# Moving one turn's older values and routing places between the two batches' scores, and one attention step ahead of the last transposes

## The chip, the cores and the metric

The kernel runs on one core of one Trainium2 chip. The metric is the device time of one execution, in microseconds (us); lower is better. The core has five engines that each take their instructions in the order in which they were written and wait for one another through semaphores: PE (TensorE, matrix products and transposes), DVE (VectorE), ACT (ScalarE), POOL (GpSimd) and SP, which here issues transfers.

## The reference

The program is a gated cross-attention block followed by a mixture of experts, for 8 batches of 256 queries, width 128, 16 heads of 64, and 1601 keys. Cut to what matters:

```python
q = (layernorm(x) @ Wq + bq)            # 16 heads of 64
k = ctx @ Wk + bk ; v = ctx @ Wv + bv
scores = q k^T / 8 ; masked ; causal    # a query sees only keys up to its own place
x = x + tanh(g_xattn) * (softmax(scores) @ v @ Wo + bo)
y = layernorm(x)
indices = argmax(softmax(y @ Wr + br))  # one expert of 8 for each token
for i in range(8):
    xi = y * (indices == i)
    out += relu(xi @ W1[i] + b1[i]) @ W2[i] + b2[i]
x = x + tanh(g_ffn) * out
```

Because of the causal mask only the first 256 keys matter (a query whose visible keys are all masked gets the mean of all values, which is why the kernel also sums the other keys).

## The kernel before

Batches are taken in 4 pairs and heads in 8 pairs, so there are `NG` = 32 turns, `g` = 0 to 31: turn `g` is pair `g // 8` of batches with pair `g % 8` of heads. Everything is float32. The loop over `g` is written out as a hand-made order (`tc.manual_schedule()`): each engine executes what the source lists, in that order, and a step that waits holds up all later steps of its engine.

One turn is spread over three passes of the loop. In pass `g` the scores of turn `g` are made; in pass `g+1` its probabilities are normalized; in pass `g+2` they are transposed and multiplied with the values. The helpers are:

- `biases(g)`: 8 small products on PE, four for each bank, that put the mask into two PSUM banks, `banks[0]` for the pair's first batch and `banks[1]` for its second (L522). They have to wait until the exponentials of turn `g-1` have read the bank.
- `scores(g, b)`: 8 source-level products on PE for batch `b` (L541, each shown twice in the trace because float32 takes two passes), then the negated row maxima on DVE: one reduction (L549) and two custom instructions (L551).
- `exps(g, b)`: four exponentials on ACT (L572), each with the reading of its row sum.
- `normalized(g, b)`: reciprocals of the row sums on DVE (L586), then two multiplications on POOL (L595).
- `turn(g, i)`: three transposes on PE (L603) into one of two PSUM buffers `pt`, and a copy out on DVE (L605). `i` is 0 to 3: batch `i // 2`, head `i % 2`.
- `values(g)`: eight products of transposed probabilities and values on PE (L616) into a PSUM buffer `o`, and for the last four turns its eviction on ACT (L637) into the tile `att` (shown as `arena`).
- `router_places(p)`: for the four 128-token tiles of a pair, 14 small bfloat16 products on PE (L716 to L720) into a buffer `n`, then five small DVE instructions (L721 to L726) that turn the counts into places of the experts' rows. `scatter` (L741) later sends rows to these places from POOL.
- `misc` is a ring of two PSUM buffers that queries, keys, values, `o`, `n` and the last outputs share.

Pass 30 (`NG - 2`) ends with `biases(30)`, `scores(30, 0)`, `exps(30, 0)`, `scores(30, 1)`, `values(28)`, `router_places(2)`. Then pass 31 begins with `turn(29, 0)`, `turn(29, 1)` and `a.out(0..3)`: the output products of the last pair for the first batch (`a`, a `Half`; the second batch is `b`), into the buffer `y_last0`, which takes the place in the ring that `o` of turn 28 has left (L779). `exps(30, 1)`, `turn(29, 2)`, `turn(29, 3)`, `normalized(30, 0)`, `normalized(30, 1)` and turn 31's own biases, scores and exponentials follow, then `values(29)`.

After the loop, `last_turns` writes out the rest. There `a.attend(g)` is `values` for one batch (L616 into the bank `sc_0`, eviction on ACT at L795), `a.out(c)` adds head pair `c`, and `plan(n)` issues the next `n` of 18 small DVE instructions (L1054) that plan the first experts' loads. It is followed by the routing of the last pair and by the experts (L986 first layer, L994 its activation, L1002 second layer, L1020 the rows' way out).

Of the kernel before, what the change touches and what calls it, by code (L numbers as in the profile page):

```python
# [53 lines left out]
def tile_gated_xattn_moe(  # L54
# [4 lines left out]
    nc = tc.nc  # L59
# [14 lines left out]
    def misc(name):  # L74
        return ps_m.tile([P, 512], F32, tag="misc", name=name)
# [188 lines left out]
    def gates():  # L264
        nc.scalar.activation(tg, g_sb, AF.Tanh)
# [213 lines left out]
    NG = NC * NPAIR  # L479
# [50 lines left out]
    def scores(g, b):  # L530

        q, k, s = qT[g], kT[g], banks[b]
        for t, at in enumerate((K0, K1)):
            for u in range(2):
                n = HB * (BLOCK[t][u] + 1)
                for j in range(2):
                    r = slice(DK * j, DK * (j + 1))
                    lo = b * S + t * P + HB * u  # L540
                    nc.tensor.matmul(  # L541
                        s[HB * u : HB * (u + 1), j, at : at + n],
                        lhsT=q[r, lo : lo + HB],
                        rhs=k[r, b * S : b * S + n],
                        start=(t == 1),
                        stop=True,
                    )
        m = nmax[g, b] = p4.tile([P, 2, 2], F32, tag="nmax", name=f"nmax_{g}_{b}")
        nc.vector.tensor_reduce(m[:, 0], s[:, :, U0:K1], AX.X, ALU.max, negate=True)  # L549
        for j in range(2):  # L550
            nc.vector.tensor_tensor_reduce(  # L551
                out=s[:, j, K1:U1],
                in0=s[:, j, K1:U1],
                in1=bias[:, 2 * (g // NC) + b],
                scale=-1.0,
                scalar=-NEG_ALL,
                op0=ALU.add,
                op1=ALU.min,
                accum_out=m[:, 1, j : j + 1],
            )  # L560
# [36 lines left out]
    def turn(g, i):  # L597

        b, j = i // 2, i % 2
        pr = prob[g, b]  # L600
        ps = ps_t.tile([P, 512], F32, tag="pt", name=f"pt_{g}_{i}")
        for n in range(3):
            nc.tensor.transpose(ps[:, n * P : (n + 1) * P], pr[:, j, K0 + n * P : K0 + (n + 1) * P], ident)  # L603
        pt = p5.tile([P, 3 * P], F32, tag="probT", name=f"probT_{g}_{i}")
        nc.vector.tensor_copy(pt, ps[:, 0 : 3 * P])  # L605
        probT[g, i] = pt
        if j == 1:
            prob.pop((g, b))
# [423 lines left out]
    def apart():  # L1032

        nc.gpsimd.memset(warm[:, 0:1], 0.0)
# [9 lines left out]
    def last_turns(a):  # L1044


        g, l = NG - 2, NG - 1
        b = Half(1, misc("y_last1")[:, 0:S], banks[0][:, 1, 0:S], banks[1][:, 1])
        steps = plan_full()

        def plan(n):
            for _ in range(min(n, len(steps))):
                f, *args = steps.pop(0)
                f(*args)  # L1054

        turn(g, 0)
        turn(g, 1)
        exps(l, 1)
        normalized(l, 0)
        scatter(10)  # L1060
        normalized(l, 1)
        scatter(11)
        apart()
        a.residual()
        a.out(NC - 4)
        plan(4)
        turn(l, 0)
        turn(l, 1)
        plan(5)
        a.attend(g, nc.scalar)  # L1070
        plan(len(steps))
        fetch_full()
        a.out(NC - 3)
        turn(g, 2)
        turn(g, 3)
        a.attend(l, nc.scalar)
        a.out(NC - 2)
        b.out(0)
        b.residual()
        a.out(NC - 1)  # L1080
        a.statistics()
        a.deviation()
        turn(l, 2)
        turn(l, 3)
        a.turned()
        b.out(1, 2)
        a.logits()
        b.attend(g, nc.vector)
        a.normalized()
        a.choice()  # L1090
        b.out(3)
        b.attend(l, nc.scalar)
        a.apply()
        b.out(4, 5)
        a.places(cb[NPAIR - 2], cb[NPAIR - 1])
        a.scatter(0)
        b.out(6, 7)
        return a, b
# [127 lines left out]
    with tc.manual_schedule():  # L1226
        plain_constants()
        for t in range(4):
            ln_stats("x0", x_sb[0], t)
        ln_scales("x0")  # L1230
        keep_awake(22)
        bias_vectors()
        prologue_c(0)
        keep_awake(3)
        prologue_apply(0)
        prologue_x(0)
        keep_awake(3)
        query(0)
        masks = [step for p in range(NPAIR) for step in [mask_bias(p)] * 4]
        mask_steps = lambda n: [next(masks.pop(0)) for _ in range(n)]  # L1240
        mask_steps(4)
        key(0, nc.vector)
        value(0)
        value(1, nc.vector)
        biases(0)
        scores(0, 0)
        exps(0, 0)
        mask_steps(4)
        scores(0, 1)
        routing_constants()  # L1250
        mean, rest_of = mean_value(), others()
        for g in range(NG):
            p, c = g // NC, g % NC
            old, new = g - 2 if g >= 2 else None, g + 1 if g + 1 < NG else None
            if g == 1:
                gates()
            if NC + 3 <= g < 2 * NC + 3:
                for i in range(2 * (g - NC - 3) + 1, min(2 * (g - NC - 3) + 3, NFILL)):
                    fill(i)
            if p >= 1 and c == 2:  # L1260
                residual(p - 1)
            if old is not None:
                turn(old, 0)
            if new is not None:
                query(new)
            if g == NC + 1:
                next(mean)
            if old is not None:
                turn(old, 1)
            if g == NG - 1:  # L1270

                o_old = misc(f"o_{old}")
                a = Half(0, misc("y_last0")[:, 0:S], banks[0][:, 0, 0:S], banks[1][:, 0])
                a.out(*range(NC - 4))
            if g > 1:
                exps(g - 1, 1, 0)
            if g > 0:
                beside_copies(p, c)
            if NC - 4 <= g < NC:
                mask_steps(2)  # L1280
            if new is not None:
                key(new)
            if g > 1:
                exps(g - 1, 1, 1)
            if g == 0:
                exps(0, 1)
            if old is not None:
                turn(old, 2)
            if 1 <= g <= NG:
                for b in range(2):  # L1290
                    normalized(g - 1, b)
            if p + 1 < NPAIR and c == 3:
                ln_scales(f"x{p + 1}")
            if g in (1, 2, 3, 5, 6):

                add_keys(g if g < 4 else g - 1)
            if g == 6:
                experts_weights()
            if p < NPAIR and c == 4:
                add_bo(p)  # L1300
            if g == NC - 1:
                join_keys()
            if g in (20, 21, 22, 24):
                next(rest_of)
            if g + 2 < NG:
                value(g + 2)
            if g == NC + 1:
                next(mean)
            beside_values(p, c)
            if old is not None:  # L1310
                turn(old, 3)
            if g == 3:
                router_constants()
            if g == 2:
                scaled()
            beside_scores(p, c)
            if g == 0:
                beside_copies(p, c)
            if g == 1:
                routing_casts()  # L1320
                more_constants()
            if g > 0:
                biases(g)
                scores(g, 0)
                exps(g, 0)
                scores(g, 1)
            if g == NC:
                next(mean)
            if old is not None:
                values(old, o_old if g == NG - 1 else None)  # L1330
            if g == NG - 3:
                router(2)
            if g == NG - 2:
                router_places(2)
            if g == 0:
                add_keys(g)
            if NC + 4 <= g < NC + 4 + E:
                other(g - NC - 4)
            if 21 <= g < 28:
                next(rest_of)  # L1340
            if g == NC + 12 + E:
                keep_weights()
            if 20 <= g < 24:
                scatter(g - 20)
            if g == NG - 2:
                residual(NPAIR - 1)
            if 26 <= g:
                scatter(g - 22)
        last_routing(*last_turns(a))
        experts()  # L1350

# [32 lines left out]
```

## Time and profile before

| what | value |
|---|---|
| median of 3 runs | 358.71 us (357.07 to 360.81) |
| time of the profiled execution | 360.69 us |
| span in its trace (first to last instruction) | 359.0 us |
| mean granted TensorE clock | 0.987 |
| PE busy / DVE / ACT / POOL | 335.5 / 243.8 / 207.6 / 215.8 us |
| PE's share of the chain of waits | 57% |

The profile page gives busy times by engine, the span in 40 slices, the DMA queues, the chain of work that ended last, and the costliest groups of instructions. The timeline lists instructions in order of time, with what ended an engine's idle time before them. Matmul records overlap, since PE is pipelined: the distance between two starts tells more than one record's length. A line of the windows view gives the length of a stretch, then busy time and number of instructions for PE, PEld (PE's weight loads), DVE, ACT and POOL, then the granted clock of PE, the DMA share and GB/s.

### The profile page before, as it was taken

The page shows a single profiled execution, that of the slowest core. Times are in us where ns is not written, and L with a number is a line of the kernel's source. Part 1 is how long each engine was busy: PE and PEld are TensorE (multiplying, and loading weights), DVE is VectorE, ACT ScalarE, POOL GpSimd, SP SyncE. Part 2 cuts the span into 40 slices and gives each one's busy share as a digit, 9 for nine tenths or more (in the row PEclk, how much of TensorE's full clock was granted, in tenths as well). Part 3 has the DMA queues.
Part 4 walks back from the last instruction along what each step waited for, and adds up shares of the span by engine and source line. Part 5 has one row for each costly group of instructions (what it writes and reads, how often), then busy time and mean ns, then how long its engine had stood idle before and what let it go on. Part 6 is the DMA issues. An engine that isn't in the chain of part 4 may idle for free.

```text
span 359.0 us, 9267 instructions
## 1 busy us (share of the span) xinstructions
PE 335.5 (93%) x3244; PEld 237.5 (66%) x3244; DVE 243.8 (68%) x857; ACT 207.6 (58%) x743; POOL 215.8 (60%) x315
## 2 busy tenths in 40 slices
PE   7978989999999999999999999999998888889993
PEld 2435646667667766666766666677666666889993
DVE  3578878785667677887766887846787775444441
ACT  3177677755555749555575665645665633356652
POOL 7065576581365777769674466594775763565553
PEclk9999999999999999999999999999999999699998
DMA  6989576796799996000000000000391017679920
GB/s 202 278 140 198 83 112 96 112 293 215 207 390 383 385 384 241 2 2 2 3 2 15 17 18 16 2 2 15 140 398 43 15 47 201 268 225 333 406 77 16
DMA packets 36471, 53.69 MB, mean 150 GB/s; under 512 B 3945, under 2 KB 22973, under 8 KB 36424
## 3 DMA queue, kind: packets, MB, share of 16 engines
q1 hardware_dynamic: 28280, 44.00, 36.2%
q0 software_dynamic: 7360, 8.73, 12.8%
q8 instruction: 26, 0.43, 0.5%
q10 hardware_dynamic: 784, 0.36, 0.3%
q14 instruction: 21, 0.17, 0.1%
HBM read 27.82 MB, written 25.71 MB: 149 GB/s over the span
## 4 chain that ended last, share of the span: by engine, by line
PE 57%; DVE 13%; DMA 11%; POOL 7%; issue 4%; ACT 4%; ACTq 1%; SPq 1%; POOLq 0%; DVEq 0%
DMA rows<-in_ctx_dram 8%; PE pt L603 8%; PE k L491 7%; PE o L616 6%; PE y L660 6%; PE hs L986 5%; DVE sc L551 5%; PE v L506 5%; PE sc L541 5%; PE ys L1002 4%; PE q L484 4%; POOL prob L595 3%; ACT prob L572 3%; PE y_last L779 2%; DVE nmax L549 2%
## 5 line engine op out<-in xcount | busy, mean ns | idle before, releaser
L572 ACT ACTIVATE prob<-sc,nmax 128x129 f32<-128x129 f32 (+1 forms) x256 | 105.2, 425 | 90.5 <-DVE nmax L551 68.7
L595 POOL TENSOR_TENSOR prob<-prob,rs 128x256 f32<-128x256 f32 (+1 forms) x128 | 102.9, 867 | 61.0 <-DVE rs L586 59.4
L603 PEld LDWEIGHTS pt<-ident,prob 128*128 128x128 f32 x384 | 46.6, 141 | 55.2 <-issue 44.6
L605 DVE COPY probT<-pt 128x384 f32<-128x384 f32 x128 | 67.2, 545 | 14.1 <-PE pt L603 13.7
L603 PE MATMUL pt<-ident,prob 128*128 128x128 f32 x384 | 64.4, 279 | 3.7 <-POOL prob L595 3.2
L551 DVE CUSTOM_DVE_ANT_0 sc<-sc,bias 128x256 f32<-128x256 f32 x128 | 55.3, 432 | 4.5 <-DVE nmax L549 0.2
L572 ACT ACTIVATION_READ_ACCUMULATOR prob<-sc,nmax 128x1 f32 x256 | 53.7, 210 | 0.0
L616 PE MATMUL o<-probT,v 128*64 128x256 f32 x480 | 45.6, 332 | 0.0
L541 PE MATMUL sc<-kT,qT 64*64 64x256 f32 (+3 forms) x1024 | 41.9, 298 | 0.0
L616 PEld LDWEIGHTS o<-probT,v 128*64 128x64 f32 x480 | 29.7, 137 | 16.7 <-issue 7.0
L491 PE MATMUL k<-cT,arena 128*128 128x512 f32 x64 | 35.5, 637 | 3.0 <-DVE arena L634 2.1
L506 PE MATMUL v<-arena,cT 128*128 128x512 f32 x64 | 33.1, 601 | 1.7 <-ACT qT L486 1.6
L484 PE MATMUL q<-xT,arena 128*128 128x512 f32 x64 | 33.1, 599 | 0.1
L541 PEld LDWEIGHTS sc<-kT,qT 64*64 64x64 f32 x1024 | 31.6, 134 | 0.1
L549 DVE TENSOR_REDUCE nmax<-sc 128x2 f32<-128x258 f32 x64 | 26.9, 420 | 4.1 <-PE sc L541 3.8
L1020 POOL DMA_INDIRECT out_dram<-o,rows x18 | 17.6, 975 | 17.5 <-DVE o L1013 13.5
L486 ACT ACTIVATE qT<-q,bqT 128x512 f32<-128x512 f32 x32 | 22.2, 693 | 9.6 <-PE q L484 9.0
L586 DVE RECIPROCAL rs<-ssum 128x4 f32<-128x4 f32 x64 | 10.9, 172 | 24.5 <-ACT prob L572 21.5
L994 ACT ACTIVATE h<-hs,arena 128x128 f32<-128x128 f32 x60 | 17.1, 368 | 15.5 <-ACT h L994 9.0
L660 PE MATMUL y<-wo_sb,arena 128*128 128x128 f32 x192 | 23.3, 276 | 0.4 <-DVE zero L370 0.2
L497 ACT ACTIVATE kT<-k,bT 128x512 f32<-128x512 f32 x31 | 21.4, 691 | 2.6 <-PE k L491 2.2
L660 PEld LDWEIGHTS y<-wo_sb,arena 128*128 128x128 f32 x192 | 22.2, 192 | 0.8 <-DVE zero L370 0.8
(242 smaller groups left out, 507.7 us busy)
## 6 DMA issues: line engine op xcount, KB each, us to landing
store<-blank SPq DMA_DIRECT2D x16, 1056.0 KB
arena<-later SPq DMA_DIRECT2D x15, 578.0 KB
rows<-in_ctx_dram POOLq DMA_DIRECT2D x5, 1024.0 KB, 9.4
later<-ws SPq DMA_DIRECT2D x1, 4624.0 KB
rows<-store SPq DMA_DIRECT2D x23, 132.0 KB
ws<-in_L_ffn_W_dram SPq DMA_DIRECT2D x1, 2048.0 KB
ws<-in_L_ffn_W_dram SPq DMA_DIRECT2D x8, 256.0 KB
rows<-in_ctx_dram SPq DMA_DIRECT2D x1, 1024.0 KB
```

What stands on the lines that cost most here:

```text
L484: nc.tensor.matmul(ps, lhsT=wq_sb[:, c * P : (c + 1) * P], rhs=xT[p], start=True, stop=True)
L491: nc.tensor.matmul(ps, lhsT=wk_sb[:, c * P : (c + 1) * P], rhs=cT[p], start=True, stop=True)
L506: nc.tensor.matmul(ps, lhsT=cT[p][:, t * P : (t + 1) * P], rhs=wv_sb[:, c * P : c * P + 512], start=True, stop=True)
L541: nc.tensor.matmul(s[HB * u : HB * (u + 1), j, at : at + n], lhsT=q[r, lo : lo + HB], rhs=k[r, b * S : b * S + n], start=(t == 1), stop=True,)
L549: nc.vector.tensor_reduce(m[:, 0], s[:, :, U0:K1], AX.X, ALU.max, negate=True)
L551: nc.vector.tensor_tensor_reduce(out=s[:, j, K1:U1], in0=s[:, j, K1:U1], in1=bias[:, 2 * (g // NC) + b], scale=-1.0, scalar=-NEG_ALL, op0= ...
L572: nc.scalar.activation(pr[:, j, lo:hi], s[:, j, lo:hi], AF.Exp, bias=m[:, t, j : j + 1], scale=-1.0 if t else 1.0, accum_out=sm[:, t, j : ...
L595: nc.gpsimd.tensor_tensor(pr[:, :, lo:hi], pr[:, :, lo:hi], r, ALU.mult)
L603: nc.tensor.transpose(ps[:, n * P : (n + 1) * P], pr[:, j, K0 + n * P : K0 + (n + 1) * P], ident)
L605: nc.vector.tensor_copy(pt, ps[:, 0 : 3 * P])
L616: nc.tensor.matmul(o[DK * j : DK * (j + 1), n * P : S], lhsT=v[:, 2 * b + n, cols], rhs=probT[g, 2 * b + j][:, 0:S] if n == 0 else probT[g ...
L660: nc.tensor.matmul(ps[:, i * D : (i + 1) * D], lhsT=attT[p * NC + c][:, t * P : (t + 1) * P], rhs=wo_sb[:, c], start=(c == 0), stop=(c == ...
```

## The change

In pass 30, `values(28)` and `router_places(2)` are issued between `scores(30, 0)` and `exps(30, 0)`, so ahead of `scores(30, 1)`, instead of behind it. In `last_turns`, `a.attend(30)` is issued ahead of `turn(31, 0)` and `turn(31, 1)` instead of behind them; `plan(5)` and `plan(len(steps))` become one call. No instruction is added, removed or resized: PE, DVE, ACT and POOL have as many as before, and SP's order is the same. On POOL only the names of operands change.

```diff
@@ last_turns
         a.residual()
         a.out(NC - 4)
         plan(4)
+        a.attend(g, nc.scalar)
         turn(l, 0)
         turn(l, 1)
-        plan(5)
-        a.attend(g, nc.scalar)
         plan(len(steps))
@@ the loop over g
                 scores(g, 0)
+                if g == NG - 2:
+                    values(old)
+                    router_places(2)
                 exps(g, 0)
                 scores(g, 1)
...
-            if old is not None:
+            if old is not None and g != NG - 2:
                 values(old, o_old if g == NG - 1 else None)
             if g == NG - 3:
                 router(2)
-            if g == NG - 2:
-                router_places(2)
```

In the instruction lists of the two programs this comes out as follows.

| engine | before | after |
|---|---|---|
| PE | scores(30,0), scores(30,1), values(28), places, turn(29,0) | scores(30,0), values(28), places, scores(30,1), turn(29,0) |
| DVE | maxima(30,0), maxima(30,1), five of places | maxima(30,0), five of places, maxima(30,1) |
| ACT | exps(30,0), eviction of values(28), exps(30,1) | eviction of values(28), exps(30,0), exps(30,1) |
| PE, later | turn(31,0), turn(31,1), attend(30), out(5) | attend(30), turn(31,0), turn(31,1), out(5) |

The DVE and ACT orders of the second part stay as they were.

## The prediction

> **What bounds the kernel now.** I read the chain of waits first, for the stretch from 274 to 295 us that the change touches; its columns are start, length and work.
>
> ```profile
> 274.62 0.25 PE sc L522 x4
> 274.87 0.59 PE sc L541 x11
> 275.49 0.44 DVE nmax L549
> ...
> 278.80 0.59 ACT arena L637
> 279.38 0.04 issue
> 279.43 2.05 PE y_last L779 x16
> 281.48 0.34 PE pt L603 x3
> ...
> 283.21 2.59 POOL prob L595 x3
> 285.80 0.16 issue
> 285.96 0.83 POOL store L741
> 286.79 0.10 issue
> ...
> 288.68 0.77 PE pt L603 x5
> 289.44 0.80 PE sc L616 x8
> 290.24 0.64 PE y_last L779 x4
> ```
>
> The chain goes from PE through the row maxima on DVE and the exponentials to the eviction of `values(28)` on ACT, back to PE (the last pair's output products), and over the normalizing on POOL to `turn(31, 0)`. No engine is full here; each is late for the next. Then I read PE's timeline, where the two holes that the change aims at stand, with what ended them in brackets, and the same seconds on ACT and DVE.
>
> ```profile
> 279.43 2.05 PE L779 MATMUL y_last<-wo_sb,arena 128*128 128x128 f32 x16 [0.86 <-ACT arena L637]
> ...
> 287.69 0.33 PE L603 MATMUL pt<-ident,prob 128*128 128x128 f32 x1 [1.09 <-POOL prob L595]
> 288.68 0.77 PE L603 MATMUL pt<-ident,prob 128*128 128x128 f32 x5 [0.66 <-POOL prob L595]
> ```
>
> ```profile
> 278.68 0.70 ACT L637 ACTIVATE arena<-o,bT 128x512 f32<-128x512 f32 x1
> 279.25 0.39 ACT L572 ACTIVATE prob<-sc,nmax 128x129 f32<-128x129 f32 x1
> ```
>
> The first hole ends with L637, because `y_last0` takes the buffer that `o` of turn 28 leaves. L637 in turn stood behind `exps(30, 0)` (from 277.08), though its data, the 16 matmuls from 275.89 with 1.52 us in all, was there at 277.41. The second hole ends with POOL.
>
> **The change, first part: values(28) and places ahead of scores(30, 1).** It costs no instruction, so I follow each engine with the lengths of the trace.
> PE: the 32 matmuls of the scores start at 274.65 and values at 275.89, so 16 of them take 0.62 us. `values(28)` then starts at 275.27 and ends at 276.79 (it needs the last `probT` copy, which ended at 275.30, only for its second half). The places took 0.36 us from start to the next start (277.35 to 277.71), so they issue from 276.72 to 277.08; `scores(30, 1)` follows to 277.70, its last result 0.2 later, 277.9. From there PE is where it was (277.71), with all the same work behind it.
> ACT: L637 runs at 276.85 instead of 278.68. `exps(30, 0)` stands behind it now and starts at 276.85 + 0.57 (278.68 to 279.25) = 277.42 instead of 277.08, so 0.34 later, ending near 279.1.
> PE again: `turn(29, 0)` and `turn(29, 1)` take 0.76 us to 278.47. L637 is done since 277.5, so the output products start at 278.47 instead of 279.43. That is a gain of 0.96 us at this place, and `turn(29, 2)` comes at 280.5 instead of 281.48.
> DVE pays. The maxima of (30, 0) end at 276.97, the places' results come at about 277.25, and their five instructions took 0.89 us from 278.15 to the start of the next at 279.04. They end near 278.15. The maxima of (30, 1), which started at 276.82, now start at 278.15: 1.33 us later. Behind them wait `exps(30, 1)` on ACT and the copies of `turn(29, 0)` and `turn(29, 1)`, which then run at 279.48 to 280.5, just ahead of the transposes that need their buffers.
> `exps(30, 1)`: from the start of the maxima to that of the exponentials it took 1.59 us for batch 0 (275.49 to 277.08), so they start at 279.74 instead of 279.25 and, with their 1.74 us, end at 281.46 instead of 280.99.
> What is late next: the second bank's biases of turn 31 wait for that end. In the lines above such a wait ended at 274.57 and DVE began its maxima at 275.49, 0.92 later. So the maxima of (31, 0) start at 281.46 + 0.92 = 282.38, against 282.98 before. Of the 0.96 us, 0.60 is left; DVE's delay takes 0.36.
>
> POOL is not the limit: the reciprocals for (30, 0) come about 1.0 us earlier, its four multiplications and one row scatter follow, and `normalized(31, 0)` then waits for its own reciprocals, so POOL gains 0.7.
>
> **Second part: attend(30) ahead of turn(31, 0).** `a.attend(30)` needs copies of `turn(30)` that end at 286.66 and `exps(31, 0)`, which end at 286.27. Moved, its 0.80 us fall into the hole before 288.68 and leave PE's list behind it. But PE is soon stopped elsewhere: DVE runs without a pause from the reciprocals at 288.58 over 18 planning steps and two copies to the copies of `turn(30, 2)` and `turn(30, 3)`, and `turn(31, 2)` needs the buffers they free.
>
> ```profile
> 288.58 0.18 DVE L586 RECIPROCAL rs<-ssum 128x4 f32<-128x4 f32 x1 [1.84 <-ACT prob L572]
> ...
> 293.73 1.01 DVE L605 COPY probT<-pt 128x384 f32<-128x384 f32 x2
> ```
>
> PE was at that point at 294.31 and started at 294.42, and its six transposes took 0.92 us there instead of the 0.76 elsewhere. So DVE sets the time, and DVE's list starts from `exps(31, 1)`, which the second part doesn't touch. I take 0 for it; its bounds are 0 and 0.80 us, the latter if DVE didn't bind.
>
> **Sum.** First part -0.60, second 0. From `turn(31, 2)` on, the same instructions follow in the same order, the first experts' loads start when the planning is through (also 0.6 earlier), and the steady experts' stage keeps its pace, so the shift reaches the end. The span goes from 359.0 to 358.4 and the profiled execution from 360.69 to 360.1. That execution lies 1.98 above the median of the runs shown; taken off the median, 358.71 - 0.60 = 358.1 us. Bounds of the working: best -0.96 - 0.80 = -1.76 (356.9). Worst, all 1.33 us of delay reach `exps(30, 1)`, which then end at 282.32 and the maxima start at 283.24, 0.26 late: 359.0.
>
> **The clock.** What can move more than that is PE's granted clock, the last figure but two in the lines of this windows view (the figures in brackets are counts).
>
> ```profile
> 301.90:305.30 3.40, 2.19 (x17) 1.72 (x16) 1.87 (x12) 1.41 (x6) 3.11 (x5) 1.00 0.84 215
> 305.30:308.70 3.40, 2.48 (x15) 2.45 (x16) 1.06 (x6) 1.27 (x5) 1.03 (x4) 0.51 1.03 414
> 308.70:312.10 3.40, 3.40 (x18) 3.40 (x18) 1.82 (x10) 0.76 (x4) 1.90 (x3) 0.50 0.60 235
> ```
>
> It is 1.00, then about a half for 6.8 us. In these, four groups of eight matmuls took 2.04, 2.06, 1.92 and 1.27 us against 1.06 at full clock, 3.05 us in all. The stretch from 284.8 to 288.2, with the second hole, was as thinly filled (PE 2.13 us of 3.40) and kept its clock. The change fills 0.8 us of it.
> [...]
>
> **Rivals.**
> 1. The gain is eaten on DVE. If the places' products take longer to arrive, or each small DVE step starts later, by 0.6 us in all, `exps(30, 1)` end at 282.07, when PE issued its biases before. Then nothing is gained: 358.7 us. For it: DVE's 1.33 us of delay is worked out, with no row of this order; against it: each step of it has a row. Chance 0.19.
> 2. Slower: the halved clock falls on the stretch from 288 to 302, where PE is busy nearly throughout. [...] Then 6.8 us at half clock do 3.4 us of work: 358.1 + 3.4 = 361.5, and two such falls in a row 364.9. [...] Chance 0.16, of which 0.10 beyond 362.3.
> 3. Faster: the work moved by 0.6 us meets the windows otherwise and the fall at 305.3 does not come. Scatter and rows then come 1.0 us earlier (2.04 against 1.06 ahead of the places) and PE's list 3.05: 355.05 to 357.1. Against: the holes ahead of it, at 302 and 305, are not touched, and the median run may lack the fall already, since it is 1.98 below the profiled one. Chance 0.17, of which 0.14 below 355.1.
>
> **How the numbers follow.** The forecast has 0.48. One per cent, 3.6 us, is about what a measurement of this kernel can tell from no change; the worked sum is a sixth of it. Faster by more has 0.14 (rival 3), slower by more 0.10 (rival 2), the same 0.76. The range goes from rival 3's 355.2 to rival 2's single fall, 361.4; the forecast alone would have 356.9 to 359.0.
>
> **What would show it.** Right: in the new trace L637 of turn 28 ahead of `exps(30, 0)`, no wait of `y_last` for ACT, the maxima of (30, 1) some 1.3 us later than (relative to 274.62) before, those of (31, 0) 0.6 earlier, `attend(30)` in the hole before `turn(31, 0)`, and PE at `turn(31, 2)` waiting longer for DVE. Wrong: second-bank biases of turn 31 that wait beyond 282.07 in these terms (rival 1), or a clock near 0.5 between 285 and 302 (rival 2).

## The result, and the profile after

| | before | after |
|---|---|---|
| median | 358.71 us (357.07 to 360.82, 19 runs) | 356.82 us (355.11 to 358.40, 19 runs) |
| ratio of the times | | 0.9951, interval 0.9935 to 0.9968 |
| profiled execution | 360.69 us | 356.23 us |
| span in its trace | 359.0 us | 354.5 us |
| mean granted clock in it | 0.987 | 0.999 |

The medians are 1.9 us apart: half a per cent, so within the 1% that counts as no change. The predicted 358.1 us lies 1.3 us above the measured median; the likeliest case's own lower end, 356.9, just misses it and the whole range holds it. Ratios, intervals and the mean clocks further down leave out executions more than 1.5% above the fastest of the same kernel (none here, one each of before on two chips and of e11, three of e12); medians are over all.

To read one trace against the other, I count from the start of the second-bank biases of turn 30 (the second L522 line of that pass). Up to there both programs issue the same instructions in the same order. It came at 274.62 us before and at 272.97 after. PE's timeline of the changed kernel from there, with what ended an idle time in brackets:

```profile
272.97 0.25 PE L522 MATMUL sc<-bias,ident_bf 64*64 64x66 bf16 x4 [1.00 <-ACT prob L572]
...
273.69 1.52 PE L616 MATMUL o<-probT,v 128*64 128x256 f32 x16
...
275.58 0.78 PE L541 MATMUL sc<-kT,qT 64*64 64x64 f32 x16
276.29 0.88 PE L603 MATMUL pt<-ident,prob 128*128 128x128 f32 x6
277.00 1.95 PE L779 MATMUL y_last<-wo_sb,arena 128*128 128x128 f32 x16
...
284.30 1.05 PE L616 MATMUL sc<-probT,v 128*64 128x256 f32 x8
285.34 0.33 PE L603 MATMUL pt<-ident,prob 128*128 128x128 f32 x1
286.33 0.77 PE L603 MATMUL pt<-ident,prob 128*128 128x128 f32 x5 [0.67 <-POOL prob L595]
...
292.07 0.92 PE L603 MATMUL pt<-ident,prob 128*128 128x128 f32 x6 [0.29 <-DVE probT L605]
```

The first hole is gone: L779 stands without a bracket. The second one, 1.09 us ahead of `turn(31, 0)`, is filled by the eight products of `attend(30)`; the 0.67 us inside that turn stay. (The float32 products stand twice in these lines: 8 in the source of L541 as 16 and the 4 of `attend(30)` as 8. The 4 bfloat16 ones of L522 for a bank stand as 4, and the transposes of L603, 3 a turn, as 3 though they are float32. Why, the trace does not tell.) And `turn(31, 2)` waits for DVE's copies, as forecast. The same place on ACT and DVE:

```profile
275.26 0.69 ACT L637 ACTIVATE arena<-o,bT 128x512 f32<-128x512 f32 x1 [2.35 <-PE o L616]
275.85 0.36 ACT L572 ACTIVATE prob<-sc,nmax 128x129 f32<-128x129 f32 x1
```

```profile
275.69 0.20 DVE L721 TENSOR_TENSOR n<-n,cb 128x32 f32<-128x32 f32 x1 [0.38 <-PE n L720]
...
276.54 0.41 DVE L549 TENSOR_REDUCE nmax<-sc 128x2 f32<-128x258 f32 x1
...
280.76 0.42 DVE L549 TENSOR_REDUCE nmax<-sc 128x2 f32<-128x258 f32 x1 [0.19 <-PE sc L541]
```

The eviction runs ahead of the exponentials, and the maxima of batch 1 stand behind the five instructions of the places. The last line is the maxima of (31, 0). In the trace of before, with its later common point, they stand at

```profile
282.98 0.43 DVE L549 TENSOR_REDUCE nmax<-sc 128x2 f32<-128x258 f32 x1
```

The chain of waits has changed its way. Over the same stretch it reads (start, length, work):

```profile
275.48 0.07 PE n L718 x3
...
276.62 0.34 DVE nmax L549
...
278.12 1.73 ACT prob L572 x8
279.85 0.04 issue
279.90 0.25 PE sc L522 x4
...
284.66 1.62 ACT prob L572 x8
286.33 0.04 issue
286.37 0.18 DVE rs L586
...
287.48 0.93 DVE probT L605 x2
...
291.47 0.47 DVE probT L605
291.94 0.14 issue
292.07 0.92 PE pt L603 x6
```

Where before went over L779 and over POOL's normalizing, it now goes over the places, the maxima of (30, 1) and their exponentials, and later over `exps(31, 1)` and DVE's planning steps to `turn(31, 2)`. Those are the two places where the prediction let DVE decide.

Set side by side, in us from the common point:

| step | before | after | moved | forecast |
|---|---|---|---|---|
| eviction of values(28), L637 | 4.06 | 2.29 | -1.77 | -1.83 |
| last pair's output products, L779 | 4.81 | 4.03 | -0.78 | -0.96 |
| maxima (30, 1) | 2.20 | 3.57 | +1.37 | +1.33 |
| exps(30, 1) | 4.63 | 5.15 | +0.52 | +0.49 |
| maxima (31, 0) | 8.36 | 7.79 | -0.57 | -0.60 |
| turn(31, 2) | 19.80 | 19.10 | -0.70 | -0.60 |
| end of the span | 84.4 | 81.5 | -2.85 | -0.60 |

So of the 4.5 us between the two spans, 1.65 arose ahead of anything that was changed, 0.70 is the new order, and some 2.1 came later. That last piece is visible in the windows views: the fall of the clock that the prediction showed at 305.3 us of before does not occur after.

```profile
301.90:305.30 3.40, 1.72 (x19) 1.50 (x17) 1.86 (x11) 2.13 (x7) 2.05 (x4) 1.00 0.96 353
305.30:308.70 3.40, 3.39 (x30) 3.17 (x29) 2.37 (x13) 2.05 (x8) 1.75 (x3) 1.00 0.88 345
308.70:312.10 3.40, 3.40 (x32) 3.38 (x31) 2.98 (x12) 2.09 (x8) 2.97 (x9) 1.00 0.23 59
```

Each line has the stretch, its length, busy time and count of PE, PEld, DVE, ACT and POOL, and the granted clock. PE is no busier in the first of them (1.72 us of 3.40, against 2.19 in before), and yet the clock stays at 1.00. The question for the experiments is therefore what makes the clock fall, and whether the change has to do with it.

### The profile page after: what moved, and what is told of

The parts are those of the page before. It is cut to its first block, busy times and chain, and to the rows that moved or that the text cites. A ratio compares the mean times of both kernels' runs of the same rounds, so it can differ in the third digit from the quotient of the medians.

```text
span 354.5 us, 9269 instructions
## 1 busy us (share of the span) xinstructions
PE 334.0 (94%) x3244; PEld 235.2 (66%) x3244; DVE 244.5 (69%) x857; ACT 208.0 (59%) x743; POOL 215.9 (61%) x315
## 4 chain that ended last, share of the span: by engine, by line
PE 61%; DVE 18%; ACT 9%; POOL 4%; issue 4%; DMA 3%; POOLq 0%; SPq 0%; DVEq 0%; ACTq 0%
PE k L491 7%; PE pt L603 7%; PE o L616 6%; DVE sc L551 6%; PE hs L986 6%; ACT prob L572 6%; PE y L660 6%; PE v L506 5%; PE sc L541 5%; PE ys L1002 5%; PE q L484 4%; DVE nmax L549 2%; DVE arena L634 2%; PE sc L522 2%; POOL prob L595 1%
## 5 line engine op out<-in xcount | busy, mean ns | idle before, releaser
L603 PEld LDWEIGHTS pt<-ident,prob 128*128 128x128 f32 x384 | 46.5, 141 | 54.0 <-issue 45.1
L603 PE MATMUL pt<-ident,prob 128*128 128x128 f32 x384 | 64.6, 279 | 1.9 <-DVE probT L605 1.1
L616 PE MATMUL o<-probT,v 128*64 128x256 f32 x480 | 45.6, 332 | 0.0
L541 PE MATMUL sc<-kT,qT 64*64 64x256 f32 (+3 forms) x1024 | 42.2, 298 | 0.0
L616 PEld LDWEIGHTS o<-probT,v 128*64 128x64 f32 x480 | 29.7, 136 | 16.8 <-issue 6.7
L541 PEld LDWEIGHTS sc<-kT,qT 64*64 64x64 f32 x1024 | 31.4, 134 | 0.1
```

The costliest lines, as they stand in the source:

```text
L541: nc.tensor.matmul(s[HB * u : HB * (u + 1), j, at : at + n], lhsT=q[r, lo : lo + HB], rhs=k[r, b * S : b * S + n], start=(t == 1), stop=True,)
L616: nc.tensor.matmul(o[DK * j : DK * (j + 1), n * P : S], lhsT=v[:, 2 * b + n, cols], rhs=probT[g, 2 * b + j][:, 0:S] if n == 0 else probT[g ...
```

## The experiments

The expectations use three theories. C: the order gives 0.6 to 0.7 us, and what is beyond it comes from falls of the clock behind PE's holes. S: the order gives all of it. A: `attend(30)` in the second hole is worth something of its own. They ran on three chips; ratios are against the kernel before on the same chip, as the record has them. They are not the quotients of the two medians (e1's would be 0.9959).

| run | median, us | before there | ratio | interval | mean clock | before's |
|---|---|---|---|---|---|---|
| e1, first part | 355.87 | 357.35 | 0.9935 | 0.9908 to 0.9961 | 0.9950 | 0.9918 |
| e2, second part | 357.23 | 357.35 | 0.9991 | 0.9968 to 1.0013 | 0.9942 | 0.9918 |
| e3, before, third hole filled | 357.07 | 357.35 | 0.9979 | 0.9958 to 1.0001 | 0.9952 | 0.9918 |
| e4, change, third hole filled | 357.03 | 357.35 | 0.9983 | 0.9957 to 1.0008 | 0.9970 | 0.9918 |
| e5, change again | 357.40 | 357.62 | 0.9995 | 0.9970 to 1.0021 | 0.9938 | 0.9922 |
| e6, before, second hole filled | 358.70 | 357.62 | 1.0029 | 1.0004 to 1.0055 | 0.9912 | 0.9922 |
| e7, change, idle products in second and third | 356.84 | 357.62 | 0.9979 | 0.9959 to 1.0000 | 0.9955 | 0.9922 |
| e8, values alone | 357.13 | 357.62 | 0.9977 | 0.9955 to 0.9999 | 0.9949 | 0.9922 |
| e9, change a third time | 363.76 | 363.69 | 0.9997 | 0.9965 to 1.0030 | 0.9824 | 0.9839 |
| e10, first part again | 362.84 | 363.69 | 0.9977 | 0.9945 to 1.0010 | 0.9847 | 0.9839 |
| e11, values alone, both filled | 363.90 | 363.69 | 1.0004 | 0.9968 to 1.0039 | 0.9865 | 0.9839 |
| e12, hole widened | 366.52 | 363.69 | 1.0079 | 1.0044 to 1.0113 | 0.9803 | 0.9839 |

What each left in its trace, from the common point (us). "Emptiest" is the least PE busy time in any 3.40 us at full clock around the second hole, found by shifting the windows view in steps of 0.2 us; "own window" is explained below the table; "half clock" tells whether the clock fell to a half right behind that hole.

| trace | maxima (31, 0) | turn(31, 2) | emptiest, us | own window, us | half clock |
|---|---|---|---|---|---|
| before | 8.36 | 19.80 | 1.65 | 2.01 | no |
| e3 | 8.35 | 21.10 | 1.64 | 1.66 | yes |
| e1 | 7.80 | 20.46 | 1.77 | 1.79 | yes |
| e10 | 7.80 | 20.42 | 1.77 | 1.78 | yes |
| e12 (widened) | 8.36 | 23.80 | 1.39 | 1.43 | yes |
| e2 | 8.36 | 19.81 | 2.16 | 2.65 | no |
| after | 7.79 | 19.10 | 2.28 | 2.30 | no |
| e4 | 7.80 | 19.12 | 2.27 | 2.53 | no |
| e5 | 7.79 | 19.11 | 2.28 | 2.41 | no |
| e9 | 7.81 | 19.13 | 2.28 | 2.29 | no |
| e6 | 8.36 | 19.82 | 2.53 | 2.55 | no |
| e7 | 7.79 | 19.44 | 2.08 | 2.10 | no |
| e8 | 7.69 | 19.07 | 2.24 | 2.42 | no |
| e11 | 7.70 | 19.41 | 2.08 | 2.33 | no |

Read in steps of 0.04 us, all changes of the clock within one trace lie on one grid of 3.413 us: in the eight traces with more than one change (before, e1, e3, e4, e9 to e12; 30 changes) none is more than 0.02 us off it. Before's are at 305.40, 312.22 and 356.60 us, 2 and 13 times 3.413 apart. In the other six traces the grid is an estimate: it is laid from their one change, near the end (353.79 in after), with the 3.413 us of the eight. e10 has seven changes, at 82.08, 85.49, 290.29, 293.70, 317.60, 324.42 and 358.56 us. The place of the grid differs between executions: the emptiest window of the grid around the second hole starts between 9.97 and 12.78 us behind the common point, at 10.79 in e1 and at 11.38 in e10, which is the same kernel.

"Own window" is PE's busy time in the emptiest window of the trace's own grid around the second hole. It sorts the table: behind the four that held 1.43 to 1.79 us the clock fell, behind the ten that held 2.01 to 2.65 it did not. Before is the case that its emptiest 1.65 us leave unexplained, since that stretch lies across the grid:

```profile
284.92:288.33 3.41, 2.01 (x13) 1.57 (x13) 1.79 (x7) 3.41 (x17) 3.22 (x4) 1.00 0.11 40
288.33:291.75 3.42, 3.07 (x27) 2.35 (x29) 2.99 (x10) 0.62 (x3) 3.07 (x5) 1.00 0.13 44
```

**e1, the first part alone.** `last_turns` is left as it was before.

```diff
                 scores(g, 0)
+                if g == NG - 2:
+                    values(old)
+                    router_places(2)
                 exps(g, 0)
```

> The first part alone: values(28) and the places between the two batches' scores, attend(30) left behind turn(31,1). Theory S (the order of the steps): counted from the start of the second-bank biases of turn 30, the maxima of (31,0) come at 7.8 us (before: 282.98 - 274.62 = 8.36; changed kernel: 280.76 - 272.97 = 7.79) and turn(31,2) at 19.1 to 19.3 (before 19.80, changed kernel 19.10): the whole of the gain by schedule is in this part, and the time is 358.1 us or 0.6 below before. Rival A (the second part is worth what the forecast lacks): turn(31,2) no earlier than 19.3, time 358.1, and 1.2 us are missing against the changed kernel. Theory C (the rest is the granted clock between 302 and 312): the time goes with the mean clock of each run, about 358.5 at 0.987 and 356.5 at 0.998, whichever part is in.

The order up to the maxima of (31, 0) is the changed kernel's (7.80), but `turn(31, 2)` comes at 20.46 instead of 19.10. PE's timeline and the windows view of e1 show why:

```profile
284.51 0.33 PE L603 MATMUL pt<-ident,prob 128*128 128x128 f32 x1 [0.97 <-POOL prob L595]
285.50 0.77 PE L603 MATMUL pt<-ident,prob 128*128 128x128 f32 x5 [0.67 <-POOL prob L595]
286.20 1.46 PE L616 MATMUL sc<-probT,v 128*64 128x256 f32 x8
287.59 1.23 PE L779 MATMUL y_last<-wo_sb,arena 128*128 128x128 f32 x4
288.61 1.38 PE L603 MATMUL pt<-ident,prob 128*128 128x128 f32 x6
289.92 0.87 PE L616 MATMUL sc<-probT,v 128*64 128x256 f32 x8
```

```profile
282.90:286.30 3.40, 1.77 (x13) 1.19 (x14) 1.49 (x7) 2.53 (x11) 3.00 (x4) 1.00 0.11 40
286.30:289.70 3.40, 3.40 (x18) 2.70 (x18) 3.12 (x13) 0.47 (x1) 3.08 (x5) 0.51 0.13 45
```

The eight products of L616 take 1.46 us, and the next eight 0.87 once the clock is back: the stretch of 3.4 us behind the unfilled hole ran at half clock. This is the prediction's second rival at its very place, but in a kernel without `attend(30)` in the hole. It costs 20.46 - 19.10 = 1.36 us there. And yet e1's time is the lowest ratio of all, 0.9935; the profiled execution is one, the others need not have fallen at that place. Theories S and A had 358.1 us, or 0.6 below before; the median is 1.48 below, and the interval is clear of the 0.998 that 0.70 us would give. The higher mean clock would account for some 0.5 us, an estimate by the rate given under e3; the rest is not explained.

**e2, the second part alone.**

```diff
         plan(4)
+        a.attend(g, nc.scalar)
         turn(l, 0)
         turn(l, 1)
-        plan(5)
-        a.attend(g, nc.scalar)
```

> The second part alone: attend(30) ahead of turn(31,0), the first part undone. Theory S: attend(30) fills the hole of PE before turn(31,0), but DVE's list decides, so turn(31,2) comes at 19.7 to 19.8 us after the start of the second-bank biases of turn 30, as before (19.80), and the time is that of before within 0.2 us, 358.7. Rival A: turn(31,2) at 19.0 and the time 357.9 or, if the part holds all of what the forecast lacks, 357.5. Theory C: the filled hole does not touch the clock after 302; the mean clocks scatter as those of before.

`turn(31, 2)` comes at 19.81, before at 19.80: nothing is gained by the order, since DVE sets that time, and the time agrees with no change. In e2's own trace, whose common point is at 271.34:

```profile
291.15 0.92 PE L603 MATMUL pt<-ident,prob 128*128 128x128 f32 x6 [0.29 <-DVE probT L605]
```

A's gain by order is refuted. S is too, as far as `turn(31, 2)`: both parts in order make 0.70 us there and no more.

**e3 and e4, products that only keep PE busy in the third hole**, ahead of the routing of the last pair, in the order of before (e3) and of the change (e4). Twelve matmuls, 1.49 us in each of the two traces, write to a bank that is overwritten later:

```diff
         turned_rows(e[2:], True)
+        for _ in range(12):
+            nc.tensor.matmul(a.y, lhsT=ones_bf, rhs=ones_bf[:, 0:1].to_broadcast([P, S]), start=True, stop=True)
         b.apply()
```

> The kernel before with 12 idle products (128x256, bfloat16, into the first half's output bank, which has been read by then) on PE in the hole between the third to fifth expert's transposes and the second expert's first layer (304.6 to 306.2 in the trace of before). They add 1.3 us of work in a hole of 1.65. Theory C: the clock no longer falls behind this hole, the mean clock is 0.997 or more in every run, and the time is 1 to 2 us below before: 356.7 to 357.7. Rival S (the clock is chance and equal in both kernels, the 1.9 us are all schedule): the time is within 0.3 us of before, whatever the clock.

> The changed kernel with the same 12 idle products in the same hole. Theory C (falls of the clock make up what the forecast lacks, and are rarer in the changed kernel): its mean clock is 0.997 or more in every run, its time 356.1 to 356.5, and it stands 0.5 to 0.9 us below the kernel before with the same products, the gain by schedule alone. Rival S: it stands the full 1.9 us below the kernel before with the products, at 356.8.

The mean clocks rise, to 0.9952 and 0.9970 from 0.9918. Over the runs of before on that chip a clock higher by 0.01 went with a time shorter by 1.52 us, so by an estimate from that rate 0.5 and 0.8 us were to be had from it; by the medians e3 and e4 gain 0.28 and 0.32 us, by the ratios 0.75 and 0.61, with intervals that reach from some 1.5 us of gain to no change. Single runs go down to 0.990 and 0.993, so C's "0.997 or more in every run" failed. So did the comparison that both theories set up: e4 should have stood 0.5 to 0.9 us (C) or 1.9 (S) below e3, and its median is 0.04 below. The 0.70 us of the order do not show in these medians, and the size of what the clock gives is not settled. In e3's trace the fall came at the other hole, which e3 leaves open: half clock from 288.25 to 291.66 us, `turn(31, 2)` at 21.10.

**e5, the change again, and e6, idle products in the second hole of before.** e5 is the changed kernel; e6 has, in the order of before:

```diff
         plan(4)
+        for _ in range(8):
+            nc.tensor.matmul(b.o, lhsT=ones_bf, rhs=ones_bf[:, 0:1].to_broadcast([P, S]), start=True, stop=True)
         turn(l, 0)
```

> The changed kernel once more, on one chip with the next three. So far the runs of the kernel before show a mean clock of 0.992 and 1.52 us per 0.01 of it, those of the changed kernel 0.995. Theory C (0.6 to 0.7 us of schedule and the rest falls of the clock): 0.995 again and 1.0 to 1.3 us below before. Rival S (all schedule): 1.9 below before at equal clock.

> The kernel before with 8 idle products (128x256, bfloat16, into the bank half that the second batch's attention overwrites later) on PE ahead of turn(31,0): 0.86 us of work in the hole that the second part of the change fills with attend(30), the order of all real steps left. Theory C (the second part's worth is that it keeps the clock up behind this hole): turn(31,2) at 19.8 us after the second-bank biases of turn 30, as before, no clock of 0.5 between 286 and 295, mean clock 0.994 to 0.996 against 0.992, time 0.3 to 0.6 us below before. Rival: the clock does not depend on this hole; 0.992 and the time of before.

e5 repeats the steps of the changed kernel to 0.02 us (`turn(31, 2)` at 19.11), but its time is only 0.22 us below that of before, ratio 0.9995. The 0.9951 of the first measurement was not found again; C had 1.0 to 1.3 us below before, S 1.9, and both missed. e6 has no half clock behind the second hole in its trace, but is slower, 1.0029, and its mean clock is no higher (0.9912); both theories had the time of before or less. As a way to gain time, filling this hole with idle products failed; what its runs lost is not known.

**e7, the change with both sets of idle products, and e8, only the values between the scores.** In e8 `router_places(2)` goes back behind `scores(30, 1)`:

```diff
                 if g == NG - 2:
                     values(old)
-                    router_places(2)
...
+            if g == NG - 2:
+                router_places(2)
```

> The changed kernel with both sets of idle products: 8 ahead of turn(31,0) and 12 in the hole behind the third to fifth expert's transposes. Theory C: every run at a mean clock of 0.997 or more (what is left falls after PE's last work), 1.5 us below before and 0.3 to 0.5 below the changed kernel, with less scatter. Rival: the falls come elsewhere instead, clock 0.995 and the time of the changed kernel.

> The change with the places left behind scores(30,1): only values(28) stands between the two batches' scores; the second part is in. In place of waiting for the places on DVE, the maxima of (30,1) wait only for PE, which comes 1.45 us later to scores(30,1). Theory S: after the second-bank biases of turn 30 the maxima of (30,1) start at 2.9 us (before 2.20, changed 3.57), exps(30,1) at 4.6 (4.63 and 5.15), the maxima of (31,0) at 7.5 (8.36 and 7.79) and turn(31,2) at 18.8 (19.80 and 19.10): 0.3 us more than the changed kernel. Rival: PE's later scores(30,1) and the two buffers of the transposes hold it, and the maxima of (31,0) stay at 7.8.

In e7 the clock is higher (0.9955) and the time about that of e4; against e5 the gain is 0.6 us with overlapping intervals. C's 0.997 in every run and 1.5 us below before did not come (lowest 0.992, and 0.8 us). The idle products did not fill the second hole here: behind `attend(30)` they waited 1.31 us for its eviction on ACT (L795), since they write to the same bank, and held `turn(31, 0)` up. The emptiest stretch there became emptier (2.08 us, after 2.28), and `turn(31, 2)` came at 19.44 instead of 19.10; e11 has the same wait, 1.32 us. In e8 the maxima of (30, 1) start at 3.02 instead of 3.57 and the exponentials at 4.61 instead of 5.15, as early as in before. But the maxima of (31, 0) come at 7.69, only 0.10 earlier than after the change, and `turn(31, 2)` at 19.07, 0.03 earlier; theory S had 7.5 and 18.8, and the rival's 7.8 is nearer. The places' steps now stand on DVE between these maxima and the copies of `turn(29, 0)` and `turn(29, 1)`, and delay the copies instead. In these two orders DVE's time for the places was paid on either side.

**e9, e10 and e11: the change, the first part, and e8 with both sets of idle products, on a third chip.**

> The changed kernel a third time, since its two measurements differ (ratio 0.9951 and 0.9995 to the kernel before). Theory C: 0.70 us of schedule and 0.002 to 0.003 more mean clock, 1.0 to 1.3 us below before. Rival D (only the schedule is there, the rest of the first measurement was chance): 0.7 us below before at the clock of before.

> The first part alone again, since only 8 runs were had. By the trace the order gains 0.55 us up to the reciprocals of (31,1). Theory C (attend(30) in the second hole matters for the clock): the mean clock is that of before, 0.992, and the time 0.5 to 0.6 us below before. Rival: the clock is 0.995 as in its first 8 runs, and the time 1.0 to 1.8 us below before, so the second part is worth nothing in any way.

> values(28) alone between the scores, attend(30) moved, and both sets of idle products. By the trace of the kernel without them the maxima of (31,0) come 0.1 us earlier than in the changed kernel. Theory C: mean clock 0.996 or more, time 1.2 to 1.5 us below before, the lowest of all variants. Rival: no better than the changed kernel.

The steps are the same again (e9: 7.81 and 19.13; e10: 7.80 and 20.42, with the half clock behind the hole as in e1). But all kernels are 5 to 6 us slower here than in the other measurements, and none of these three differs from before by more than its interval. Of the forecasts, e9's 1.0 to 1.3 us (C) and 0.7 (D) below before, and e11's clock of 0.996 and lowest time of all, did not come (e9 is 0.07 us above before, e11 0.21). The first part alone (e10) has a lower median than the whole change (e9), by 0.92 us with overlapping intervals. PE's timeline of e9 shows a fall that the other chips' traces do not have:

```profile
313.43 0.30 PE L977 MATMUL hs<-ident,rows 128*128 128x128 f32 x1 [0.25 <-PE ys L1002]
317.46 2.08 PE L986 MATMUL hs<-xsT,ws 128*128 128x128 f32 x8 [3.73 <-DVE xsT L979]
```

PE waits 3.73 us for the sixth expert's rows, and behind that its eight matmuls take 2.08 us (1.16 in the traces of the other chips). In e11 they take 2.08 and in e10 2.07. A gain of 0.7 us cannot be read against that.

**e12, the hole made wider.** In the order of before, two more instructions on POOL, 2.17 us together, ahead of the normalizing of turn 31:

```diff
         exps(l, 1)
+        for _ in range(2):
+            nc.gpsimd.tensor_tensor(blank[:, 0:512], blank[:, 0:512], blank[:, 0:512], ALU.add)
         normalized(l, 0)
```

> The kernel before with two additions of 128x512 (about 1.3 us each on POOL, into a tile that is no longer read) ahead of normalized(31,0), so that PE's hole ahead of turn(31,0) grows by some 2.6 us to over 4 us. Theory C (a fall of the clock follows thin windows of PE): behind the hole the clock is 0.5 for 3.4 or 6.8 us in nearly every run, mean clock 0.983 to 0.988, time 4 to 6 us above before, of which 2.6 are the additions. Rival (falls are chance, not tied to PE's holes): mean clock 0.992, time 2.6 us above before or less.

`turn(31, 0)` comes at 15.19 us instead of 13.07, that is 2.1 later, and PE's wait grows from 1.09 to 3.21 us:

```profile
288.73 0.47 PE L603 MATMUL pt<-ident,prob 128*128 128x128 f32 x1 [3.21 <-POOL prob L595]
289.74 1.33 PE L603 MATMUL pt<-ident,prob 128*128 128x128 f32 x5 [0.53 <-POOL prob L595]
291.00 1.55 PE L616 MATMUL sc<-probT,v 128*64 128x256 f32 x8
```

```profile
283.80:287.20 3.40, 1.73 (x14) 1.48 (x12) 1.83 (x7) 3.40 (x17) 3.13 (x4) 1.00 0.11 40
287.20:290.60 3.40, 1.34 (x5) 1.05 (x6) 2.29 (x6) 0.21 (x2) 3.24 (x4) 0.55 0.00 0
290.60:294.00 3.40, 3.40 (x18) 2.36 (x17) 3.06 (x11) 0.47 (x1) 3.00 (x5) 0.50 0.14 45
294.00:297.40 3.40, 3.40 (x28) 2.86 (x27) 1.68 (x7) 0.47 (x1) 0.00 (x0) 0.95 0.12 42
```

The clock is a half for two such windows, the one with the hole and the next. `turn(31, 2)` comes 4.0 us later than before, of which 2.1 is the hole and 1.9 came in the stretch at half clock. So in this trace a fall came behind an emptier hole, and cost about as much as the hole itself; with the table above, this is the firmest evidence for C. The run times decide less. The mean clock is lower than that of before on the chip (0.9803 against 0.9839; single runs from 0.964 to 0.989, before's from 0.977 to 0.994), but the median is only 2.83 us longer. C had 4 to 6 us and the rival 2.6 or less, with 2.6 for the two additions, which held `turn(31, 0)` up by only 2.1. Taking off the 2.1 leaves 0.7 us for the clock, so a fall of this size in nearly every run, as C had it, is not shown.

## Why the prediction was right, and where it was not

- **First part, -0.60 us: right.** Up to the maxima of (31, 0) each step came within 0.2 us of its forecast, in the seven traces that hold the first part whole (after, e1, e4, e5, e7, e9, e10). The output products gained 0.78 instead of 0.96 us: `scores(30, 1)` started 2.61 us after the common point, where the working had 277.08 - 274.62 = 2.46, and took 0.71 to the next start where it had 0.62. DVE's delay then took back 0.21 instead of 0.36, so that 0.57 was left of the forecast's 0.60.
- **"From `turn(31, 2)` on the shift stays": 0.70 instead of 0.60.** The reciprocals ahead of the planning steps start 0.56 us earlier, and from there to `turn(31, 2)` it takes 5.70 us instead of 5.84. One of them, which makes `tri_full`, took 0.23 us instead of 0.40; the trace does not tell why. That the shift reaches the end fits, but is not proven: of the traces without half clock before PE's last work and without idle products in the third hole, e2 and e6 (no first part) end 82.0 and 82.5 us behind the common point, after and e5 (the change) 81.5 and 81.4.
- **Second part, 0: right by order, too narrow as a price.** e2 shows the 0 (19.81 against 19.80). What this step missed is the clock behind the hole that the moved products fill. With the hole open, three of the four traces that were not widened fell behind it (e1, e3, e10; not before) and lost 1.3 to 1.4 us at `turn(31, 2)`; with it filled, none of nine. For an execution that falls there, the bounds "0 and 0.80 us" should have gone to 1.36 and beyond. How often executions fall there is not known, and the run times do not show this price: the first part alone, with the hole open, has a lower ratio than the whole change both times that it ran (0.9935 and 0.9977, against 0.9951, 0.9995 and 0.9997). The prediction had all that was needed: it showed the hole, and said that the change fills 0.8 us of it. But it gave the half clock behind that hole to a rival, as a loss by the change, not to the second part's price.
- **Rival 1** (the gain eaten on DVE) did not come: its sign, biases of turn 31 at 282.07 or later in before's terms, would have been 7.45 us from the common point, and after the change the chain has them at 279.90, that is 6.93. The gain stood.
- **Rival 2** (half clock on the stretch from 288 to 302) named the right place, but it occurs where the change has *not* filled the hole. In the five traces of the changed order (after, e4, e5, e7, e9) it never occurred; their own windows there held 2.10 to 2.53 us of PE's work.
- **Rival 3** (the fall at 305.3 does not come) is what the profiled execution shows, and it brought some 2.1 us; the prediction had 1.0 to 3.05. The windows that this rival speaks of were found as the grid of 3.413 us under the table of traces. But the missing fall cannot be put down to the shift: of the other 13 traces none has half clock from 22 to 37 us behind the common point, though nine of them leave the holes there open, and two of these, e2 and e6, have no shift either (`turn(31, 2)` at 19.81 and 19.82). Nor does the filling of the windows tell them apart: before's own window from 301.99 us held 2.10 us of PE's work and was followed by the fall, after's from 302.58 held as much and was not. The prediction's own caution, that the median run may lack it already, was the better reading.
- **End to end.** The change was measured three times: 0.9951, 0.9995 and 0.9997. The 0.70 us that the traces share would be 0.998; the last two intervals hold it, the first ends below. What made up the further 1.2 us of the first measurement is open; the clocks of before's runs there are not on record, but for the profiled one. That 356.82 lies inside the stated range is owed to the width that rival 3 gave it, not to the sum. Two things that scatter by as much are known: the clock (among the runs of before on two chips some 1.5 us for 0.01), and the way to the common point, which took 271.3 to 275.5 us in the 14 traces though it is the same program. Between the two profiled executions, 1.64 of the 1.65 us stood already at 54 us, behind a stretch in which the chain of waits of before spends 10.27 us on one load of context rows.

## What to carry to other kernels

When a moved step fills a hole on PE, price it twice: by the order (what waits for what behind it) and by the clock. Here the first price was 0. The second was 1.3 us in three traces that left the hole open, though no difference of medians shows it; the clock was a half behind the four holes whose own window held 1.43 to 1.79 us of PE's work, and not behind the ten with 2.01 to 2.65.

When two profiled executions are compared, fix a common point ahead of the first changed instruction and count from there: the steps then repeat to 0.03 us where the clock is the same, while the executions differ by 4 us for reasons that have nothing to do with the change. A gain of 0.2% is found in this way and not by medians.

## What was unexpected in the hardware

PE's clock fell behind stretches that were far from empty. The 3.40 us ahead of e1's fall held 1.77 us of PE's work, and the widest gap in them was 0.97 us. In the traces the changes lie on a grid of 3.413 us, at another place in each execution, and the order of before was followed by a half clock at the second hole where one window of the grid took in most of the hole (1.66 us of PE's work in e3), and not where the grid cut it in two (2.01 and 3.07 in before). Around that hole the windows that were followed by a half clock held up to 1.79 us, the others 2.01 or more. Elsewhere in the traces this does not hold: a window of the grid with 2.10 us came ahead of a fall (before, from 301.99) and one with 1.74 did not (after, from 346.95). Nor did a busy window always keep the clock: e4 and e10 fell at 80.43 and 82.08 us behind a window in which PE was busy throughout, but for some 1.9 us of it with sixteen products of a single column (L400, 128x1). What makes the clock fall, no run here shows. The half clock behind this hole lasted one window, 3.4 us, in e1, e3 and e10 and two, 6.8 us, in e12; before's from 305.40 lasted two. These two went on behind a first window in which PE was busy for 1.68 us (e12) and 2.59 (before); all five ended behind one in which PE was busy throughout.
